# Loading the first adapter factors and one weight chunk of a fused LoRA and FFN kernel in other pieces, on other queues

## The chip, the cores and the metric

The kernel runs on 1 core of one Trainium2 chip. The metric is the device time of the whole program in microseconds (us). The kernel before took 473.98 us, the median of 3 runs (473.75 to 474.29).

## The reference

For each of 8 batches of 256 tokens with 1024 features, a low-rank adapter chosen by an index is applied, its result goes through a feed-forward network whose inputs are rounded to fp8, and the input is added back:

```python
Bx  = einsum('bni,bri->bnr', x, B[ids])        # rank 16
h   = einsum('bnr,bor->bno', Bx, A[ids])
g   = fp8(h) @ gate_w.T ;  u = fp8(h) @ up_w.T  # 1024 -> 2752
out = x + fp8(silu(g) * u) @ down_w.T           # 2752 -> 1024
```

## The kernel before

**Tiling.** The 2048 tokens are four blocks of 512 (t = 0 to 3), each of two batches. Features are eight groups of 128 (k = 0 to 7). The 2752 hidden features are 22 chunks (c = 0 to 21) of 128. TensorE takes a 128x128 piece of weights and streams 512 tokens past it: 16 such matmuls for one chunk and one block (eight k for gate, eight for up).

**Start.** While the first transfers are under way TensorE multiplies ones (`warm`, L523). Block 0 goes first: `two_times_b` (L549) makes `bx` = B x, eight matmuls for each k, in the order of k; two small `warm` matmuls stand before k 7 and six behind it. VectorE and ScalarE copy `bx` to `bm`. `two_times_a` (L618) makes `c` = A `bm` in 32 short matmuls of 32 rows for each half, and both engines round `c` to fp8 as `xg`. Then `gate_up(0, 0)` runs, and from there on TensorE goes from chunk to chunk.

**What is loaded, and in which order.** Nearly all loads are issued by SyncE (SP); a few by ScalarE (ACT) and GpSimd (POOL). x of block 0 comes in four pieces: k 0 and 1, k 2 to 4, k 5 and 6, k 7 (L432, L433, L441, L442). B of batch 0 goes out on ScalarE's queue (L434), B of batch 1 on SP (L440). `touched` (L436) is a 1 KB read of the weights into a scrap tile. A of the two batches goes into one tile, `a_two[0]`, whose 128 rows are cleared by GpSimd (L384): `load_a_two` (L398) brings 48 rows of 2 KB for each batch, 16 rows for one half of the output, 16 rows that the host has filled with zeros, and 16 rows for the other half. Both go out on SP behind all of x. Then come gate and up weights, 1 MB for each chunk: chunks 0 and 1 in two halves, 2 to 4 whole (L445).

**Block 1.** Seven chunks (0 to 6) are used first for block 0 alone. There are five weight buffers, so chunk 5 is loaded when chunk 0's buffer is free and chunk 6 when chunk 1's is. Chunk 6 is loaded in two halves with all of block 1's x between them: half of chunk 6 (L770 to L772), x k 0 to 6 (1792 KB), x k 7 (256 KB), the other half. In chunk 6 the rows stand gate k 0 to 7, then up k 0 to 7 (`GATE_FIRST`). `gate_up(6, 0)` runs the gate matmuls of k 0 to 3 first; then `two_times_b_in_parts` makes `bx` of block 1 (L790), which needs block 1's x; then come gate k 4 and 5, up, and so on. x of blocks 2 and 3 (2 MB each) and their A and B follow on SP.

**Later.** For the other blocks chunks 0 and 1 are loaded again, and chunks 7 to 21. `NSPLIT = 3` makes chunks 7, 8 and 9 come in two halves.

**Queues.** An engine issues its instructions in order. The program uses eight completion semaphores for the DMAs of SP and ScalarE, in turn: a DMA that takes one again first waits until the DMA that had it has landed.

Of the kernel before, what the change touches and what calls it, by code (L numbers as in the profile page):

```python
# [23 lines left out]
H = 1024  # L24
I = 2752
R = 16
NH = H // P
# [7 lines left out]
NAHEAD = 2  # L35
NHELD = NFIRST + NAHEAD

NSPLIT = 3

GATE_FIRST = (1, NHELD - 1)  # L40

# [25 lines left out]
def x_of(x4, t, k):  # L67

    first = 0
    for n in PIECES[t]:  # L70
        if k < first + n:
            break
        first += n
    at = (t * NH + first) * P * TB
    piece = x4[at : at + n * P * TB].rearrange("(p k n) -> p k n", p=P, k=n)
    return piece, first
# [18 lines left out]
def gate_up_of(w_gu, c):  # L95
    at = c * 2 * NH * P * P
    return w_gu[at : at + 2 * NH * P * rows_of(c)].rearrange("(p n) -> p n", p=P)
# [204 lines left out]
def adaln_ffn(  # L302
# [15 lines left out]
    nc = tc.nc  # L318
# [45 lines left out]
    with ExitStack() as fast:  # L364
# [5 lines left out]
        xs = [acts.tile([P, NH, TB], F32, name=f"x{t}") for t in range(NTB)]  # L370
# [8 lines left out]
        b_two = [lora.tile([P, 2 * BROW + R], F32, name=f"b{t}") for t in range(2)]  # L379
        a_two = [lora.tile([P, H // 2], F32, name=f"a{t}") for t in range(2)]  # L380
# [7 lines left out]
        def adapter_of(batch, queue):  # L388
            return queue.value_load(ids_i[0:1, batch : batch + 1], min_val=0, max_val=7)  # L389

        def load_b(b, i, adapter, queue):
            load = queue.dma_start(  # L392
                out=b[:, i * BROW : (i + 1) * BROW], in_=b8[bass.ds(adapter * P, P), :]
            )
            if queue is nc.gpsimd:
                tc.keep_in_program_order(load)

        def load_a_two(j, adapter):  # L398
            row = 2 * 32 * j + R * j
            nc.sync.dma_start(  # L400
                out=a_two[0][row : row + 3 * R], in_=a8[bass.ds(adapter * 3 * R, 3 * R), :]
            )

        def load_a_twice(a, q, src, part, queue):
            load = queue.dma_start(
# [5 lines left out]
        def load_x(t, k):  # L411
            piece, first = x_of(x4, t, k)
            ks = slice(first, first + piece.shape[1])
            nc.sync.dma_start(out=xs[t][:, ks, :], in_=piece)  # L414

        w_of = {}

        def load_gate_up(c, parts=1, between=()):
            n = NH if c == NI - 1 else 2 * NH
            w = wpool.tile([P, 2 * NH, P], F32, tag="w", name="w_gu")[:, :n]  # L420
            src = gate_up_of(w_gu, c).rearrange("p (k n) -> p k n", n=P)
            n //= parts
            for i in range(parts):
                nc.sync.dma_start(out=w[:, bass.ts(i, n)], in_=src[:, bass.ts(i, n)])  # L424
                if i == 0:
                    for load in between:
                        load()
            w_of[c] = w
# [2 lines left out]

        load_x(0, 0)  # L432
        load_x(0, 2)  # L433
        load_b(b_two[0], 0, adapter_of(0, nc.scalar), nc.scalar)  # L434
        touched = const.tile([R, R], F32, name="touched")
        nc.scalar.dma_start(  # L436
            out=touched, in_=gate_up_of(w_gu, 0).rearrange("(r g) n -> r g n", r=R)[:, 0, :R]
        )
        second = adapter_of(1, nc.sync)
        load_b(b_two[0], 1, second, nc.sync)  # L440
        load_x(0, 5)  # L441
        load_x(0, 7)  # L442
        load_a_two(1, second)
        load_a_two(0, adapter_of(0, nc.sync))
        for c in range(NFIRST):  # L445
            load_gate_up(c, parts=2 if c < 2 else 1)
        adapters = [adapter_of(2 + q, nc.gpsimd if q < 2 else nc.sync) for q in range(6)]
        lane = const.tile([P, 1], I32, name="lane")
        nc.gpsimd.iota(lane, pattern=[[0, 1]], base=0, channel_multiplier=1)
# [127 lines left out]
        def two_times_b_in_parts():  # L577

            n = SEQ // 2
            bx = [psum.tile([P, n], F32, tag="ps", name=f"bx{half}") for half in range(2)]
            times_b([bx[q // 2] for q in range(4)], b_twice[0], n, quads_of_two(1))
            bm = lora.tile([P, 2, n], F32R, name="bm_parts")
            rest = in_place_of_hid(NI - 11, [P, 2, n], F32R, "rest")
            held = tc.keep_in_program_order
            own = [slice(64 * half, 64 * (half + 1)) for half in range(2)]
            for half, copy in enumerate((nc.vector.tensor_copy, nc.scalar.copy)):
                held(copy(bm[own[half], half], bx[half][own[half]]))
            for half in range(2):  # L590
                held(
                    nc.vector.tensor_tensor(
                        rest[own[half], half],
                        bx[half][own[half]],
                        bm[own[half], half].bitcast(F32),
                        ALU.subtract,
                    )
                )
            for part, half in ((bm, 1), (bm, 0), (rest, 0), (rest, 1)):
                held(nc.scalar.copy(part[own[1 - half], half], part[own[half], half].bitcast(F32)))  # L600
            return [part.rearrange("p h n -> p (h n)") for part in (bm, rest)]
# [52 lines left out]
        def two_times_a_part(bms, part):  # L654
            round_two(1, part, times_a_parts(bms, a_parts[0], 2 * part), cut=1 + part)
# [11 lines left out]
        def four_times_a(bms, i):  # L667
            cs = times_a_parts(bms, a_parts[1 + i // 2], 2 * (i % 2))
            for q in range(4):
                to = xg[2 + q // 2][:, 2 * i : 2 * i + 2, bass.ts(q % 2, SEQ)]  # L670
                round_to(to, cs[q], nc.vector if q % 2 else nc.scalar)
# [81 lines left out]
        two_times_a(bm)  # L753
        gate_up(0, 0, turns=(2, 2, 2, 2))
        load_gate_up(NFIRST)
        tc.keep_in_program_order(nc.gpsimd.tensor_copy(b_two[1][:1, :1], w_of[2][:1, 0, :1]))
        for j in range(2):
# [10 lines left out]
        for c in range(NFIRST + 1, NHELD - 1):  # L768
            load_gate_up(c)
        load_gate_up(  # L770
            NHELD - 1, parts=2, between=(lambda: load_x(1, 0), lambda: load_x(1, NH - 1))
        )  # L772
        for t in (2, 3):
            load_x(t, 0)
# [8 lines left out]
        for c in range(2, NHELD - 1):  # L783
# [5 lines left out]
            between={  # L789
                4: lambda: bms.append(two_times_b_in_parts()),  # L790
                10: lambda: two_times_a_part(bms[0], 0),
            },
        )
        gate_up(NAHEAD, 1, turns=(4, 1, 1, 1, 1), between={5: lambda: two_times_a_part(bms[0], 1)})
        for c in range(NAHEAD + 1, NHELD - 2):
# [7 lines left out]
            between={  # L803
                8: lambda: four_times_a(bms[1], 2),
                14: lambda: four_times_a(bms[1], 3),
            },
# [2 lines left out]
            for t in (2, 3):  # L809
                gate_up(c, t)  # L810
        for c in (*range(NAHEAD), *range(NHELD, NI)):
            load_gate_up(c, parts=2 if NHELD <= c < NHELD + NSPLIT else 1)
            if c == NI - 2:
                nc.sync.dma_start(out=wt, in_=w_d_tail)
            for t in range(1 if c < NAHEAD else 0, NTB):
                gate_up(c, t)
# [71 lines left out]
        for k in range(NH - 1):  # L888
# [23 lines left out]
            first = k % 2 == 0  # L912
# [133 lines left out]
```

## Time and profile before

| | us |
|---|---|
| median of 3 runs | 473.98 |
| lowest, highest | 473.75, 474.29 |
| the profiled execution's own time | 473.92 |
| its span | 472.3 |
| TensorE busy in the span | 467.6 (99%) |
| VectorE, ScalarE, GpSimd busy | 106.6, 194.8, 16.0 |

The span runs from the first to the last instruction that the profiler saw. Engines are PE (TensorE matmuls), PEld (TensorE weight loads), DVE (VectorE), ACT (ScalarE), POOL (GpSimd) and SP (SyncE); a "q" behind an engine's name stands for its instruction queue, which is where DMAs are issued. Times in views are microseconds from the start of the span. An entry such as "[0.28 <-DMA x<-x]" says that the engine sat idle for 0.28 us and that a transfer of x ended that.

### The profile page before, as it was taken

The page shows a single profiled execution, that of the slowest core. Times are in us where ns is not written, and L with a number is a line of the kernel's source. Part 1 is how long each engine was busy: PE and PEld are TensorE (multiplying, and loading weights), DVE is VectorE, ACT ScalarE, POOL GpSimd, SP SyncE. Part 2 cuts the span into 40 slices and gives each one's busy share as a digit, 9 for nine tenths or more (in the row PEclk, how much of TensorE's full clock was granted, in tenths as well). Part 3 has the DMA queues.
Part 4 walks back from the last instruction along what each step waited for, and adds up shares of the span by engine and source line. Part 5 has one row for each costly group of instructions (what it writes and reads, how often), then busy time and mean ns, then how long its engine had stood idle before and what let it go on. Part 6 is the DMA issues. An engine that isn't in the chain of part 4 may idle for free.

```text
span 472.3 us, 5980 instructions
## 1 busy us (share of the span) xinstructions
PE 467.6 (99%) x2477; PEld 214.6 (45%) x2477; DVE 106.6 (23%) x170; ACT 194.8 (41%) x257; POOL 16.0 (3%) x32
## 2 busy tenths in 40 slices
PE   8999999999999999999999999999999999999997
PEld 5444444444444444444444444444444444444444
DVE  2314341222121212212122121231120111031031
ACT  2315258996655655453345545359112012021000
POOL 0230500000000000000000000000000000000000
PEclk9999999999999999999999999999999999999999
DMA  8999105352222201222221011132425345153031
GB/s 304 421 381 358 48 3 161 109 176 89 90 89 90 89 24 67 89 90 89 90 85 23 26 62 57 61 105 103 142 109 161 76 175 162 42 207 103 3 116 68
DMA packets 14661, 56.01 MB, mean 119 GB/s; under 512 B 1762, under 2 KB 2786, under 8 KB 12066
## 3 DMA queue, kind: packets, MB, share of 16 engines
q1 hardware_dynamic: 14256, 55.08, 34.0%
q8 instruction: 21, 0.34, 0.3%
q0 software_dynamic: 192, 0.40, 0.3%
q14 instruction: 14, 0.11, 0.1%
q10 hardware_dynamic: 178, 0.07, 0.1%
HBM read 47.15 MB, written 8.39 MB: 118 GB/s over the span
## 4 chain that ended last, share of the span: by engine, by line
PE 94%; DMA 4%; SPq 0%; issue 0%; DVE 0%
PE y L521 60%; PE yd L521 32%; DMA x<-x 4%; PE c L521 1%; PE bx L521 1%; DMA ids_i<-ids 0%; SPq L389 0%; PE warm L521 0%; SPq L392 0%; SPq L414 0%; DVE o L853 0%; SPq L424 0%; PE count L521 0%
## 5 line engine op out<-in xcount | busy, mean ns | idle before, releaser
L521 PE MATMUL y<-xg,w_gu 128*128 128x512 fp8e4 x1376 | 298.6, 379 | 0.0
L521 PEld LDWEIGHTS <-w_gu 128*128 128x128 bf16 x1376 | 133.7, 98 | 162.1 <-DVE xg L606 1.6
L521 PE MATMUL yd<-hid,w_d 128*128 128x512 fp8e4 (+2 forms) x693 | 146.0, 373 | 0.0
L695 ACT ACTIVATE g<-y,gate_s 128x512 f32<-128x512 f32 (+1 forms) x88 | 59.5, 681 | 134.1 <-PE y L521 134.1
L724 DVE SCALAR_TENSOR_TENSOR hid<-y,up_by_down,g 128x512 fp8e4<-128x512 f32 x84 | 63.1, 751 | 215.8 <-PE y L521 145.7
L521 PEld LDWEIGHTS <-w_d 128*128 128x128 bf16 x693 | 66.6, 98 | 78.9 <-issue 1.7
L507 ACT ACTIVATE junk<-w_d 128x1408 bf16<-128x1408 uint16 (+1 forms) x16 | 21.2, 1324 | 88.5 <-DMA w_d<-w_d 88.4
L853 DVE SCALAR_TENSOR_TENSOR o<-yd,down_s,x 128x512 f32<-128x512 f32 x28 | 20.0, 747 | 107.5 <-PE yd L521 93.9
L507 ACT ACTIVATE junk<-w_gu 128x2048 bf16<-128x2048 uint16 (+1 forms) x22 | 41.0, 1864 | 0.0
L514 ACT ACTIVATE junk<-hid 128x2048 bf16<-128x2048 fp8e4 x21 | 40.1, 1908 | 0.6
L514 ACT ACTIVATE junk<-xg 128x2048 bf16<-128x2048 fp8e4 x8 | 15.3, 1910 | 0.3
L606 DVE TENSOR_SCALAR xg<-c,inv 128x512 fp8e4<-128x512 f32 (+1 forms) x20 | 11.7, 638 | 6.4 <-PE c L521 6.4
L608 ACT ACTIVATE xg<-c,inv 128x512 fp8e4<-128x512 f32 (+1 forms) x20 | 10.6, 601 | 4.5 <-PE c L521 4.5
L521 PE MATMUL warm<-const-bfloat16-1.0 128*128 128x512 bf16 (+1 forms) x22 | 6.0, 430 | 0.9 <-PEq L1035 0.9
L853 DVE SCALAR_TENSOR_TENSOR o<-yd,down_s,xg 128x512 f32<-128x512 f32 (+2 forms) x5 | 3.2, 644 | 12.2 <-PE yd L521 9.8
L521 PEld LDWEIGHTS <-const-bfloat16-1.0 128*128 128x128 bf16 x23 | 2.3, 118 | 4.3 <-issue 4.0
L507 ACT ACTIVATION_READ_ACCUMULATOR junk<-w_gu 128x1 f32 x22 | 4.2, 193 | 0.0
L521 PE MATMUL yd<-hid_tail,w_dt 64*128 64x512 bf16 (+1 forms) x32 | 4.2, 377 | 0.0
L724 DVE SCALAR_TENSOR_TENSOR tail<-y,up_by_down,g 64x512 fp8e4<-64x512 f32 x4 | 3.0, 756 | 4.9 <-ACT g L695 4.8
L514 ACT ACTIVATION_READ_ACCUMULATOR junk<-hid 128x1 f32 x21 | 3.9, 187 | 0.0
L521 PE MATMUL bx<-x,b_four_twice 128*32 128x256 f32 x64 | 3.7, 381 | 0.0
L460 POOL TENSOR_SCALAR a_parts<-a_four,minus 128x512 fp32r<-128x512 f32 x2 | 3.1, 1564 | 1.7 <-DMA a_four<-a_twice 1.7
(69 smaller groups left out, 55.5 us busy)
## 6 DMA issues: line engine op xcount, KB each, us to landing
w_gu<-w_gu SPq DMA_DIRECT2D x17, 1024.0 KB, 4.9
outT<-o SPq DMA_DIRECT2D x31, 256.0 KB, 2.1
w_gu<-w_gu SPq DMA_DIRECT2D x13, 512.0 KB, 5.1
w_d<-w_d SPq DMA_DIRECT2D x8, 704.0 KB, 5.1
w_d<-w_d SPq DMA_DIRECT2D x8, 640.0 KB, 3.9
x<-x SPq DMA_DIRECT2D x2, 2048.0 KB, 20.0
x<-x SPq DMA_DIRECT2D x1, 1792.0 KB, 14.4
x<-x SPq DMA_DIRECT2D x2, 512.0 KB, 3.8
```

The source lines that it names most:

```text
L460: held(engine.tensor_scalar(parts, a, minus, None, ALU.mult))
L507: nc.scalar.activation(junk_like(w), low(w), AF.Copy, accum_out=lows[:rows, column : column + 1])
L514: nc.scalar.activation(junk_like(q), q, AF.Square, accum_out=squares[:rows, column : column + 1])
L521: tc.keep_in_program_order(nc.tensor.matmul(*args, **kwargs))
L606: nc.vector.tensor_scalar(to, c, scale, None, ALU.mult, saturate=False)
L608: nc.scalar.activation(to, c, AF.Copy, scale=scale, saturate=False)
L695: nc.scalar.activation(g[rows], gates, AF.Silu, scale=gate_s[: gates.shape[0]])
L724: nc.vector.scalar_tensor_tensor(to, in0=ups, scalar=up_by_down[rows], in1=g[rows], op0=ALU.mult, op1=ALU.mult, saturate=False,)
L853: nc.vector.scalar_tensor_tensor(o, in0=y, scalar=down_s, in1=x, op0=ALU.mult, op1=ALU.add)
```

## The change

`load_a_two` now brings only the rows that are not zero: two loads of 16 rows (32 KB) for each batch, in place of one of 48 rows (96 KB). The two of batch 1 stay on SP behind all of x. The two of batch 0 go out on ScalarE's queue, behind a one-element copy on ScalarE that reads x at k 2, and so waits for the piece k 2 to 4. SP no longer reads batch 0's index. Chunk 6 is loaded in three parts: a quarter (gate k 0 to 3), block 1's x, a quarter (gate k 4 to 7), then the half with up. Chunks 7 to 9 are loaded whole.

```diff
-NSPLIT = 3
+NSPLIT = 0
...
-        def load_a_two(j, adapter):
-            row = 2 * 32 * j + R * j
-            nc.sync.dma_start(
-                out=a_two[0][row : row + 3 * R], in_=a8[bass.ds(adapter * 3 * R, 3 * R), :]
-            )
+        def load_a_two(j, adapter, queue):
+            for g in range(2):
+                row = 32 * (2 * j + g) + R * j
+                tc.keep_in_program_order(
+                    queue.dma_start(
+                        out=a_two[0][row : row + R],
+                        in_=a8[bass.ds(adapter * 2 * R + g * R, R), :],
+                    )
+                )
...
-        def load_gate_up(c, parts=1, between=()):
+        def load_gate_up(c, parts=(0, 4), between=()):
...
-            n //= parts
-            for i in range(parts):
-                nc.sync.dma_start(out=w[:, bass.ts(i, n)], in_=src[:, bass.ts(i, n)])
+            cuts = [n * i // 4 for i in parts]
+            for i, at in enumerate(zip(cuts[:-1], cuts[1:])):
+                nc.sync.dma_start(out=w[:, slice(*at)], in_=src[:, slice(*at)])
                 if i == 0:
                     for load in between:
                         load()
...
-        load_b(b_two[0], 0, adapter_of(0, nc.scalar), nc.scalar)
+        first = adapter_of(0, nc.scalar)
+        load_b(b_two[0], 0, first, nc.scalar)
...
-        load_a_two(1, second)
-        load_a_two(0, adapter_of(0, nc.sync))
+        load_a_two(1, second, nc.sync)
+        tc.keep_in_program_order(nc.scalar.copy(touched[:1, :1], xs[0][:1, 2, :1]))
+        load_a_two(0, first, nc.scalar)
         for c in range(NFIRST):
-            load_gate_up(c, parts=2 if c < 2 else 1)
+            load_gate_up(c, parts=(0, 2, 4) if c < 2 else (0, 4))
...
         load_gate_up(
-            NHELD - 1, parts=2, between=(lambda: load_x(1, 0), lambda: load_x(1, NH - 1))
+            NHELD - 1,
+            parts=(0, 1, 2, 4),
+            between=(lambda: load_x(1, 0), lambda: load_x(1, NH - 1)),
         )
...
-            load_gate_up(c, parts=2 if NHELD <= c < NHELD + NSPLIT else 1)
+            load_gate_up(c, parts=(0, 2, 4) if NHELD <= c < NHELD + NSPLIT else (0, 4))
...
-        "a8": np.insert(a8, 1, 0, axis=1).reshape(8 * 3 * R, H // 2),
+        "a8": a8.reshape(8 * 2 * R, H // 2),
```

## Prediction

> **What bounds the kernel now.** I read the page's first part, then who makes TensorE wait, then the chain that ended last, then the first 45 us in order of time.
>
> ```profile
> PE 467.6 (99%) x2477; PEld 214.6 (45%) x2477; DVE 106.6 (23%) x170; ACT 194.8 (41%) x257; POOL 16.0 (3%) x32
> ```
>
> ```profile
> PE warm L521 <- PEq L1035: 0.9, 1, 0.9
> PE bx L521 <- DMA b<-b: 0.4, 1, 0.4
> PE bx L521 <- DMA x<-x: 0.3, 1, 0.3
> ```
>
> PE is busy 467.6 of 472.3 us, and in the waits it waits three times in all, 1.6 us. So the change has little to take. From the chain:
>
> ```profile
> 3.94 4.86 DMA x<-x
> 8.80 0.04 issue
> 8.84 0.43 PE bx L521 x8
> 9.27 0.46 PE warm L521 x6
> 9.72 0.04 issue
> 9.77 2.19 PE c L521 x61
> 11.96 7.03 PE y L521 x32
> ...
> 19.37 14.42 DMA x<-x
> 33.79 0.14 issue
> 33.93 1.96 PE bx L521 x64
> ```
>
> Two transfers are in it. The first is k 7 of block 0's x (landed 3.94 + 4.86 = 8.80). The second is the large piece of block 1's x (landed 19.37 + 14.42 = 33.79), and there PE stood, as its own order of time shows:
>
> ```profile
> 11.89 21.76 PE L521 MATMUL y<-xg,w_gu 128*128 128x512 fp8e4 x100
> 33.93 1.96 PE L521 MATMUL bx<-x,b_twice 128*32 128x128 f32 x64 [0.28 <-DMA x<-x]
> 35.81 1.47 PE L521 MATMUL y<-xg,w_gu 128*128 128x512 fp8e4 x6
> ```
>
> From 11.89 to 33.65 there are 100 matmuls at 0.218 us each and no gap; then 0.28 us idle for x. That figure hides a little, since a matmul's end is modelled. From the start of the last y (33.27) to that of the first bx (33.93) there are 0.66 us; at 50.45, where bx follows y without a wait, there are 0.31 (50.15 to 50.46). So x's lateness costs 0.35 us. After it no wait of PE is listed to the end.
>
> **The change part by part, against the profiled execution's 473.92 us.**
>
> *Chunk 6 in three.* Ahead of block 1's x stand 256 KB less of chunk 6. The DMA engines are full in this stretch:
>
> ```profile
> 19.40:33.80 14.40, 14.25 (x67) 6.26 (x64) 3.43 (x5) 2.75 (x4) 7.12 (x12) 1.00 1.03 389
> ```
>
> The last two columns are the DMA share (1.03) and GB/s (389). The piece was issued at 19.37 and took 14.42 us because of what stood before it in SP's queue. 262 KB at 389 GB/s are 0.67 us; the 64 KB of zero rows that go (2 x 16 rows of 2 KB) are another 0.17. So x lands at 33.79 - 0.84 = 32.95. PE wants it at 33.93 - 0.35 = 33.58. The stall of 0.35 goes entirely, with 0.6 us to spare. What is late next? The second quarter of chunk 6 (gate k 4 and on) is wanted when bx ends, about 35.5. The old second half was issued at 20.33 and landed 15.4 later at 35.73; the quarter now ends 256 KB and 64 KB sooner, 34.9. The up half lands at 35.73 - 0.17 = 35.56; it is wanted after gate k 4 to 7, 35.5 + 4 x 0.22 = 36.3. Both hold, with 0.6 to 0.8 us in hand. If that cover is gone (a slow DMA engine), each 0.1 us late is 0.1 us of stall. **-0.35 us.**
>
> *SP's later issues.* One more part moves each later DMA one semaphore on. x of block 2 now waits for chunk 3 in place of chunk 2, block 3's for chunk 6's first quarter in place of chunk 5 (27.63 before, about 29 now), and its B for block 1's x (about 33). At each of these moments the queue still holds more than the 2 MB of block 2 (landing 20.80 + 19.9 = 40.7), so the engines don't run dry and nothing lands later. The next to need them are GpSimd's copies, which end at 49.05 for a bx at 50.45: 1.4 us of cover, 0.35 of which the gain eats. **0.**
>
> *Start: x.* SP's issues through k 7 of x stay. The two loads on ScalarE's queue put 64 KB beside x. If both get ahead of x's k 7, that is two rows of 2 KB on each of 16 engines: 64 KB at 371 GB/s (the rate from 2 to 8.5 us) are 0.17 us, and k 7 is on the chain, one for one. Bounds 0 and +0.17; I take **+0.05**, since k 7 was issued at 3.94 and these can't be before 6.2.
>
> *Start: A.* Here is the risk. Today A is issued on SP at 4.64 and 5.80 and takes
>
> ```profile
> L400 SPq DMA_DIRECT2D a<-a x2: 330/342/355, 4.6 to 5.8; - x2
> ...
> DMA to landing us min/median/max: 3.8/3.8/3.8
> ```
>
> so the later one lands at 9.63, just before c starts at 9.77. But `warm` runs until 9.72 and the copies to `bm` end at 9.58 (VectorE) and 9.62 (ScalarE), so an earlier A gains at most 0.1 us. How late may it be? The list of the changed program's instructions with their waits shows what the loads wait for. On SP the first takes the semaphore that x k 2 to 4 had, which landed 4.85 after 1.29, at 6.14; so it goes out at 6.17 in place of 4.64, the second at about 6.55. On ScalarE the copy waits for the same x. I place the two issues at about 6.2 and 6.6 (one issue takes 0.35 to 0.39 there). Behind them on ScalarE stands only the copy to `bm` at 9.36. The price of such a load, from both sides: an output write in a quiet queue lands 2.0 us after issue, so 8.6; on ScalarE's queue under x's traffic B took 3.4 and `touched` 3.6, so 10.0 to 10.2; A on SP took 3.83, so 10.43. PE would start c late by 0 to 0.3, 0.5 or 0.7 us. The nearest rows are those of ScalarE's queue, and I go below them for a reason that the trace shows. `touched` and B had their first packets 2.65 and 2.30 us after issue, where a load in a quiet queue has it after 0.97 (the loads from 78.99 on); the rest, 1.68 and 1.33, is a wait behind x packets of 4 and 6 KB at 159 and 234 ns, some 6 to 9 packets. Now the packets in front are x's 2 KB at 84 ns: 0.5 to 0.75 us. So the last load's packets start at 6.6 + 0.97 + 0.65 = 8.2, and first packet to landing took 0.94 and 1.06 for those two rows: 9.2. On SP the two loads follow k 7 directly, with a third of the old rows each, and land by about 9.3. Gain or loss at c: **0** (bounds -0.1 to +0.7).
>
> The DMA page of the Trainium skill speaks against this part ("DMA: Bandwidth & Descriptors", section "Rules for kernel authors"): loads under 64 KB pay mostly overhead and should be joined, and spreading DMAs over queues wins no bandwidth. By that, four loads of 32 KB in place of two of 96 KB would save nothing of the 0.17 us, and the sum would be -0.13 in place of -0.30. The same page ("Queues, rings and completion order") has each DMA engine serve its queues in turn, one packet of several descriptors at a time, so that a load on ScalarE's queue would wait for at most what one SP packet holds; the waits of `touched` and B fit that, and by it A lands in time.
>
> *Start: weights.* SP's first weight loads are held up too. The first half of chunk 0 goes from 6.17 to about 6.95; chunk 1's first half waits for k 5 and 6 of x (3.46 + 4.38 = 7.84), its second for a ScalarE load (about 9, before 7.59), chunks 2 to 4 come 1 to 2 us later. What hides it: the engines still work off x and A until 8.4. Half of chunk 0 landed at 11.2 and is wanted at 11.9. Chunk 1's second half landed at 7.59 + 8.5 = 16.1 and is wanted after 24 matmuls, 11.89 + 24 x 0.218 = 17.1; its data can't start before chunk 0 and chunk 1's first half (1.5 MB, until about 12.5) are through, so an issue at 9.6 is early enough. Without that cover the price would be the 1 us by which a delay of 2 us oversteps 17.1. **0.**
>
> *The rest.* Chunks 7 to 9 whole: the first is loaded at 86 us and used after chunks 0 and 1 of three blocks (about 129), so nothing. The copy of one element and two more DMA issues lie on ScalarE's idle 6.65 us before 9.36. **0.**
>
> Sum: -0.35 + 0.05 = -0.30. 473.92 - 0.30 = 473.62; the median of the runs is 0.06 above the profiled one, so 473.7.
>
> **Rivals.**
>
> *A lands late, and c waits* (slower). One mechanism: the second ScalarE load, issued at 6.6, takes as long as rows of that queue did. The start loses what the load comes in after 9.7. The gain of 0.30 is used up at a landing of about 10.0, 3.4 us after issue, which is B's own time. At 3.6 it is 10.2: +0.5 - 0.3 = +0.2, 474.2. At the 4.86 us of x's k 7, 11.46: +1.75 - 0.3, 475.4. For it: two rows of the very queue. Against: packets in front are a third as long, and 32 KB is less than B's 68.
>
> *The stall stays* (the change doesn't do what it says). One of 16 DMA engines ends far behind the others at block 1's x: the first of its 16 completions came at 32.09, the last at 33.79. If that engine's lag comes from something other than bytes, x lands no earlier and only the start's +0.05 is left: 474.0. Against: its queue is served in order, and it too has 16 KB less before x.
>
> *A little more*: the stall goes, A comes 0.1 earlier and x is not touched: 473.92 - 0.45 = 473.5.
>
> **Chances.** Forecast 0.55, A late 0.22, the stall stays 0.13, a little more 0.10. Range: low end 473.5 less the 0.2 by which runs lie below the median; high end 473.92 - 0.35 + 0.17 + 0.7 = 474.4, rounded up to 474.5. A measurement of this kernel can tell about 0.2% (0.95 us) from no change. Faster by more needs 473.0, where no part reaches: 0.04. Slower by more needs 474.9, A about 1.2 us late: 0.08, out of the first rival. Same: 0.88.
>
> **What would show it.** In the changed profile: PE without a wait for x before block 1's bx, which starts at about 33.6; c starting at 9.8; the A loads landing before 9.7; y starting at 11.9 to 12.0; the second quarter and half of chunk 6 not waited for. A wait of c for A would prove the first rival, a wait of bx for x near 33.7 the second. I am wrong if PE waits anywhere that it doesn't today.

## The result and the profile after

The changed kernel takes 475.19 us (median of 22 runs, 474.29 to 476.45) where the kernel before took 474.08 (22 runs, 473.65 to 474.82). The ratio is 1.0021, with a 95% interval from 1.0015 to 1.0027. So the change costs about 1.1 us; the forecast was 473.7, and the time lies above its range, which ended at 474.5.

The profiled execution of the changed kernel took 474.52 us, near the low end of its runs, with a span of 472.6. Its totals look like those of before. First line of the page:

```profile
PE 468.1 (99%) x2477; PEld 214.6 (45%) x2477; DVE 106.6 (23%) x170; ACT 195.2 (41%) x258; POOL 16.0 (3%) x32
```

What makes TensorE wait (total us, times, longest):

```profile
PE warm L527 <- PEq L1043: 0.9, 1, 0.9
PE bx L527 <- DMA x<-x: 0.3, 1, 0.3
```

The wait for x that is left is that of block 0's k 7. The one for block 1's x, 0.28 us in the prediction's lines, is no longer listed. But x is not early: it landed at 34.01, where 32.95 was forecast, and bx started 0.16 us later, at 34.17. (Where bx does wait for it, it starts 0.13 to 0.14 us behind x's landing, 33.79 and 33.93 before.) And the chain that ended last (start, us, what) tells of something new:

```profile
1.30 4.94 DMA x<-x
...
6.26 0.07 ACT touched L449
...
6.43 3.18 DMA a<-a
...
9.63 0.33 SPq L428
...
10.01 9.34 DMA w_gu<-w_gu
...
19.39 14.85 PE y L527 x68
34.24 1.89 PE bx L527 x64
```

The old chain went through two loads of x. The new one goes through a weight load: chunk 2, issued at 10.01, landed at 19.34, and y of chunk 2 started right behind it. TensorE's own order of time shows no bracket at that place, because the wait is short and the end of a matmul is modelled:

```profile
12.21 22.03 PE L527 MATMUL y<-xg,w_gu 128*128 128x512 fp8e4 x100
34.17 1.96 PE L527 MATMUL bx<-x,b_twice 128*32 128x128 f32 x64
```

The starts tell it. Where nothing waits, the 100 matmuls need 21.69 us from the first y to block 1's first bx (this is so in six of the kernels below). Here it is 34.17 - 12.21 = 21.96: 0.27 us were lost at chunk 2. Before it was 22.04, 0.35 lost at x. The 0.27 are not a price of chunk 2 alone: had it come in time, x would still have held bx until about 34.15, by the 0.14 us above.

A second profile of the changed kernel (after_again below; 474.99 us) shows the same wait at a size that no one misses; x landed at 34.56 there, again just ahead of bx:

```profile
11.97 7.28 PE L527 MATMUL y<-xg,w_gu 128*128 128x512 fp8e4 x32
19.83 14.85 PE L527 MATMUL y<-xg,w_gu 128*128 128x512 fp8e4 x68 [0.58 <-DMA w_gu<-w_gu]
34.69 1.95 PE L527 MATMUL bx<-x,b_twice 128*32 128x128 f32 x64
```

From block 1's bx on the four profiles of the two kernels are equal to 0.02 us: 16.53 us to block 2's bx (which is that of block 3 too), 269.19 to the first `yd`, 149.43 to the last matmul. So in them one number holds what the change does inside the span: when block 1's bx starts. It is 33.93 and 33.64 in two profiles of before, 34.17 and 34.70 in two of after, 0.65 us later on average. Both profiles of after are quicker than most of its runs: the median span of the 22 is 473.3, against 472.25 to 472.5 in the medians of the runs of before made with the experiments. One more place where the time can go is shown by after_padded, below.

Another 0.25 us of the 1.1 lies outside the span: the time less the span is 1.80 to 2.01 us in the 22 runs of after, 1.90 in the median, and 1.65 to 1.68 in the medians of the runs of before. Among the experiments, those with A on ScalarE's queue and chunk 6 in three have it too (touched_on_pool, ungated, early_w, after_padded: 1.85 to 1.88); a_only has 1.71, and all others, c6_only and a_on_sp among them, have 1.64 to 1.73. No view shows what that is.

**Where the weights became late.** SP's own order of time, before:

```profile
4.64 1.49 SPq L400 DMA_DIRECT2D a<-a  x2
6.17 3.62 SPq L424 DMA_DIRECT2D w_gu<-w_gu  x7
```

and after:

```profile
3.94 0.43 SPq L418 DMA_DIRECT2D x<-x  x1
6.37 0.91 SPq L402 DMA_DIRECT2D a<-a  x2
7.33 4.79 SPq L428 DMA_DIRECT2D w_gu<-w_gu  x7
```

SP stands from 4.37 to 6.3 for the semaphore of x k 2 to 4, then issues two A loads, and only then the first weights: at 7.33 in place of 6.17. What that does to the DMA engines is seen in the stretch from 6 to 16 us, which the view cuts into 40 slices of 0.25 us; each digit is the busy share of the 16 engines in tenths. Before:

```profile
DMA  9989899999999799999999999999999999998899
DMA packets 1090, 3.85 MB, mean 385 GB/s; under 512 B 132, under 2 KB 140, under 8 KB 991
```

After:

```profile
DMA  7979999998699999987899993946969999999989
DMA packets 1029, 3.27 MB, mean 327 GB/s; under 512 B 162, under 2 KB 176, under 8 KB 992
```

Before, the engines are full nearly from end to end (7 tenths once, at 9.25). After, they have holes at 8.25 to 8.75 (8 and 6 tenths) and at 12.0 to 13.5 (down to 3 tenths), and in ten microseconds 0.58 MB less came in. Only 0.06 MB of that is the zero rows that A no longer brings. The other 0.52 MB is 1.35 us of transfer at the 385 GB/s of before, an estimate from these two lines. It is early weights. Everything behind them in SP's queue comes later for it: chunk 2, where TensorE first runs into the hole, and block 1's x behind that.

### The profile page after: what moved, and what is told of

Read it like the earlier page. It is cut to its first block, busy times and chain, and to the rows that moved or that the text cites. A ratio compares the mean times of both kernels' runs of the same rounds, so it can differ in the third digit from the quotient of the medians.

```text
span 472.6 us, 5984 instructions
## 1 busy us (share of the span) xinstructions
PE 468.1 (99%) x2477; PEld 214.6 (45%) x2477; DVE 106.6 (23%) x170; ACT 195.2 (41%) x258; POOL 16.0 (3%) x32
## 4 chain that ended last, share of the span: by engine, by line
PE 95%; DMA 4%; SPq 0%; DVE 0%; issue 0%; ACT 0%; ACTq 0%
PE y L527 62%; PE yd L527 32%; DMA w_gu<-w_gu 2%; PE bx L527 1%; DMA x<-x 1%; PE c L527 1%; DMA a<-a 1%; SPq L418 0%; DVE o L861 0%; SPq L428 0%; ACT touched L449 0%; ACTq L402 0%; PE count L527 0%
```

## The experiments

The theories that the runs were to tell apart:

- *The turn of the semaphores.* Two more DMAs on SP's and ScalarE's turn of eight put SP's first A load behind x k 2 to 4, and all weights behind that. Late weights make y wait, wherever A is.
- *ScalarE's queue.* A, or x k 7 beside it, comes late because two loads go on another queue than SP's, and c starts late.
- *The later issues.* Not the first weight load but chunk 1's second half and chunk 2, which wait for semaphores until 9.6 and 10.0, are too late.
- *Smaller loads, or where A lies.* Four loads of 32 KB are slow in themselves, or A's smaller tensor moves the other tensors in memory.

### Which half of the change costs: c6_only, a_only

c6_only is the kernel before with chunk 6 in three parts and nothing else. a_only is the changed kernel with chunk 6 in two halves and chunks 7 to 9 split again.

```diff
# c6_only, against before
... (load_gate_up takes the cuts, as in the change)
-            NHELD - 1, parts=2, between=(lambda: load_x(1, 0), lambda: load_x(1, NH - 1))
+            NHELD - 1, parts=(0, 1, 2, 4), between=(lambda: load_x(1, 0), lambda: load_x(1, NH - 1))
# a_only, against after
-NSPLIT = 0
+NSPLIT = 3
-            parts=(0, 1, 2, 4),
+            parts=(0, 2, 4),
```

> The kernel before with only chunk 6 in three (a quarter, block 1's x, a quarter, a half); A's loads and chunks 7 to 9 as before. Theory 1 (A's loads on ScalarE's queue make x's k 7 and A late) and theory 2 (the weight loads, issued up to 2 us later because their semaphores come from A's loads, make chunk 2 late): 473.7, that is 0.35 under before, with no wait of bx for x near 33.6. Rival 3 (the quarters of chunk 6, with 2 KB rows, or their place, are what costs): 474.6 or more, with a new wait behind 33.6.

> The changed kernel with chunk 6 in two halves and chunks 7 to 9 in halves, as before: A's part of the change alone. Theories 1 and 2: as slow as the changed kernel, 475.0 to 475.6; the wait of bx for block 1's x is there only as far as TensorE isn't late already. Rival 3: 474.1 or less.

c6_only: 474.38 us, ratio 1.0003 [0.9994, 1.0012]. a_only: 475.12, ratio 1.0023 [1.0014, 1.0032]. The whole loss is in the loads of A and what they move. In c6_only's profile there is no wait at block 1's bx (21.69 us from the first y), so the third part does what was forecast at that place; that it wins nothing measurable is taken up with before_again.

### Does ScalarE's queue cost: a_on_sp

All four A loads on SP, without the copy.

```diff
-        tc.keep_in_program_order(nc.scalar.copy(touched[:1, :1], xs[0][:1, 2, :1]))
-        load_a_two(0, first, nc.scalar)
+        load_a_two(0, adapter_of(0, nc.sync), nc.sync)
```

> The changed kernel with all four A loads on SP behind all of x, batch 1's first, and no copy on ScalarE. Theory 1: x's k 7 lands at 8.8 again, c starts at 9.8, and the time falls by 0.3 to 1 us, to 474.2 or under. Theory 2: chunk 1's second half and chunk 2 now wait for x's k 7 and the first A load, so they go out near 8.9 and 9.3 in place of 9.6 and 10.0 (before: 7.6 and 8.1); most of the loss stays, 474.6 to 475.1, as a wait for chunk 2 near 19.

475.11 us, ratio 1.0018 [1.0009, 1.0027], as slow as the change. Chunk 0 was issued at 7.29 here too. So the queue of batch 0's A isn't the cause of the loss inside the span (the 0.25 outside it is absent here). The chain that ended last goes through block 1's x again and not through a weight load:

```profile
19.71 14.70 DMA x<-x
34.41 0.14 issue
34.55 1.96 PE bx L526 x64
```

Of the 0.63 us lost between the first y and this bx, about 0.2 lie in front of chunk 2 and about 0.4 in front of bx. The start of c, which I had suspected, also falls: it is 10.09 after, but 10.07 in c6_only, whose start is that of before, and 9.83 in after_again. It moves with x k 7's landing (8.80 to 9.20 among these), and in c6_only with A's (9.94), from run to run.

### How much do profiles of one kernel differ: after_again, before_again

The two kernels as they are, profiled once more, without an edit.

> The changed kernel once more, for a second profile. Its runs lie between 474.3 and 476.5, and the first profile is of a quick one (474.52). Theory 1: c starts at 10.0 to 10.2 again. Theory 2: the wait for chunk 2 near 19 is there again and is the part that varies from run to run: 0.3 us to 2 us.

> The kernel before, for a second profile. Theory 2 (SP's later weight issues are what costs): weights' packets at about 160 ns from chunk 0's second half on, chunk 1's second half begins near 12.8 to 12.9, no wait of y; bx of block 1 at 33.8 to 34.0. If it shows slow packets in chunk 1 too, as the changed kernel does, they don't come from the change.

after_again: 474.99 us; 1.03 us lost between first y and block 1's bx, most of it at chunk 2 (the fence above). before_again: 473.62 us; 21.71 us from the first y to block 1's bx, so the stall of 0.35 that the forecast meant to win is hardly there (0.02). In this execution x landed at 33.50, and y ended when it did. The stall is a matter of the execution, not of every one. In c6_only's profile, whose 474.38 is the median of its runs, there is none, but c started 0.30 us later than in before's, which takes back most of what that wins. Whether the third part has to do with the later start isn't shown; nothing is issued differently up to there.

### Are the later issues the cause: hold_sp

The kernel before with a copy of 64 bytes on SP between the halves of chunk 1, which waits for x k 7. It leaves chunk 0 and chunk 1's first half where they were and holds the rest up as the change does.

```diff
+        held_at = const.tile([1, 16], F32, name="held_at")
+        def hold():
+            tc.keep_in_program_order(
+                nc.sync.dma_start(out=held_at, in_=xs[0][:1, NH - 1, :16])
+            )
-            load_gate_up(c, parts=2 if c < 2 else 1)
+            load_gate_up(c, parts=2 if c < 2 else 1, between=(hold,) if c == 1 else ())
```

> The kernel before, with one added 64-byte copy on SP between the halves of chunk 1, which waits for x's k 7; its result isn't used. A is untouched, SP issues chunk 1's second half at about 9.2 and chunk 2 at 9.7, as in the changed kernel, while chunk 0 and chunk 1's first half go out as before. Theory 2: 474.7 to 475.3, with y waiting near 17 or 19. Theory 1 (A's loads themselves, or ScalarE's queue): 474.0 to 474.3, and no wait of y.

Chunk 0 was issued at 6.21, chunk 1's second half at 9.59, chunk 2 at 10.20 (after: 7.33, 9.63, 10.01). Chunk 2 landed at 18.49, on time, and 21.77 us lie between y and bx. So in this execution the later issues opened no hole. The median is 474.62, ratio 1.0019 [1.0010, 1.0029]; the medians alone stand 1.0012 apart. The profile can't explain those 0.6 us, since it is of the quickest of the ten runs (474.21); they lie inside the span (472.95 in the median, before 472.35). This run doesn't take the later issues' part of the loss to nothing; ungated, below, speaks to it again.

### Late weights without touching A: dummy_two, two_on_sp

The kernel before, with A's loads as they were. dummy_two adds the copy and two 1 KB loads on ScalarE's queue, so that the turn of the semaphores is that of the change or worse (A itself goes out at 6.36 and 7.52 here, in place of 4.64 and 5.80). two_on_sp adds two 1 KB loads on SP between A and the weights.

```diff
# dummy_two, against before
+        tc.keep_in_program_order(nc.scalar.copy(touched[:1, :1], xs[0][:1, 2, :1]))
+        for i in range(2):
...
+                nc.scalar.dma_start(
+                    out=scrap,
+                    in_=gate_up_of(w_gu, 0).rearrange("(r g) n -> r g n", r=R)[:, 1 + i, :R],
+                )
# two_on_sp, against before
... (first is the index of batch 0, read as before)
+        for i in range(2):
+            scrap = const.tile([R, R], F32, name=f"scrap{i}")
+            tc.keep_in_program_order(
+                nc.sync.dma_start(
+                    out=scrap, in_=a8[bass.ds(first * 3 * R + 2 * R * i, R), :R]
+                )
+            )
```

> The kernel before, A's two loads of 48 rows on SP included, with the changed kernel's one-element copy and two more 1 KB reads of the weights on ScalarE's queue in the place of A's; their results aren't used. They shift the turn of the eight semaphores as the change does. Theory 2: SP issues chunk 0 at 7.3 and chunk 2 at 9.5 or later, and the time is 474.7 to 475.4. Theory 1: 474.0 to 474.3.

> The kernel before with two more loads on SP, of 1 KB each, between A's second load and chunk 0; their results aren't used. A's loads, queues and sizes are as before. SP issues chunk 0's first half at about 7.2 in place of 6.2, as in the changed kernel. Theory 5 (what costs is that chunk 0's first half goes out late, 7.3 in place of 6.2: the cold start of the weights' stream then isn't covered by x and A, and chunks 0 and 1 come about 1 us later): 474.8 to 475.3, chunk 1's second half begins at 13.7 or later in place of 12.8. If it is A's loads in their new form or on ScalarE's queue: 474.0 to 474.3.

dummy_two: 475.67 us, ratio 1.0040 [1.0026, 1.0054], chunk 0 issued at 7.90. two_on_sp: 475.68, ratio 1.0028 [1.0015, 1.0040]. SP in two_on_sp:

```profile
4.63 1.49 SPq L400 DMA_DIRECT2D a<-a  x2
6.33 0.85 SPq L449 DMA_DIRECT2D scrap<-a  x2
7.22 4.03 SPq L424 DMA_DIRECT2D w_gu<-w_gu  x7
```

A goes out when it always did; the weights go out 1.05 us later for two DMAs of 1 KB. And TensorE pays at y and at bx:

```profile
12.53 21.76 PE L529 MATMUL y<-xg,w_gu 128*128 128x512 fp8e4 x100 [0.54 <-DMA w_gu<-w_gu]
35.46 1.95 PE L529 MATMUL bx<-x,b_twice 128*32 128x128 f32 x64 [1.17 <-DMA x<-x]
```

The delay of the first weights alone, with A's loads where they were, makes a loss of the same kind and at least the same size. The bytes lost at 8 to 15 us come due at the first piece that TensorE needs soon (chunk 0 here, chunk 2 in the change) and at block 1's x behind them.

### The change with the old issue times: a0_on_pool, pool_later

Batch 0's two A loads on GpSimd's queue, which doesn't take part in the turn of the eight semaphores. In pool_later they stand behind a one-element copy that reads x k 0.

```diff
# a0_on_pool, against after
-        tc.keep_in_program_order(nc.scalar.copy(touched[:1, :1], xs[0][:1, 2, :1]))
-        load_a_two(0, first, nc.scalar)
+        load_a_two(0, adapter_of(0, nc.gpsimd), nc.gpsimd)
# pool_later, against after
-        tc.keep_in_program_order(nc.scalar.copy(touched[:1, :1], xs[0][:1, 2, :1]))
-        load_a_two(0, first, nc.scalar)
+        zeroth = adapter_of(0, nc.gpsimd)
+        seen = const.tile([1, 1], F32, name="seen")
+        tc.keep_in_program_order(nc.gpsimd.tensor_copy(seen, xs[0][:1, 0, :1]))
+        load_a_two(0, zeroth, nc.gpsimd)
```

> The changed kernel with batch 0's two A loads on GpSimd's queue, which has semaphores of its own, and no copy on ScalarE; SP's loads then take the semaphores that they had before, and are issued at the old times, chunk 2 at about 8. Theory 2: the loss is gone, 473.7 to 474.2, no wait of y; only x may come up to 0.2 later, since these loads go out near 3.5, ahead of x's k 5 to 7. Theory 1 (it is the loads of 16 rows, on whichever queue): 474.8 or more.

> The change with batch 0's two A loads on GpSimd's queue, behind a one-element copy on GpSimd of x k 0 (so that they go out at about 4.5 to 5, behind x's own issues, where they went out at 3.64 and 4.34 and held x k 7 up by 0.74 us before). Theory of the semaphores' turn: SP and ScalarE have the old count of DMAs, so chunk 0's first half is issued at 6.1 to 6.3, chunk 2 lands by 18.7, y runs into block 1's bx without a stall (21.7 us); x k 7 lands near 8.85, c starts at 9.8 to 10.1, bx of block 1 at 33.6 to 33.9: 473.6 to 474.2, ratio 0.999 to 1.0005. If the start of c is later still because A itself comes late on this queue, c starts above 10.3 and the time is 474.4 or more. Rival (four small loads cost the time wherever they are): 475, ratio 1.002.

a0_on_pool: 474.16 us, ratio 0.9999 [0.9989, 1.0009]. pool_later: 474.08, ratio 1.0003 [0.9994, 1.0012]. Both issue chunk 0 at 6.18 to 6.19, and neither has a wait between y and bx. The DMA engines in pool_later, 6 to 16 us, are full again:

```profile
DMA  9999899999899699999999999989999999999899
DMA packets 1095, 3.78 MB, mean 378 GB/s; under 512 B 164, under 2 KB 178, under 8 KB 996
```

Four small loads are not the cost, then. But they don't pay either. In a0_on_pool they went out at 3.64 and 4.34 and ran ahead of x k 7, which landed at 9.54 in place of 8.80, and c started 0.66 late; in pool_later they went out at 4.97 and 5.67, x k 7 landed at 9.12, c started 0.25 late. What they saved at bx (0.35) is spent there, wholly in a0_on_pool and for the greater part in pool_later.

### Where A lies in memory: after_padded, before_short

after_padded gives the changed kernel an A tensor of the old size, 768 KB. before_short gives the kernel before one of 512 KB (its loads then start at other rows, so that their contents are not those of A).

```diff
# after_padded, against after
-        "a8": a8.reshape(8 * 2 * R, H // 2),
+        "a8": np.pad(a8.reshape(8 * 2 * R, H // 2), ((0, 8 * R), (0, 0))),
# before_short, against before
-                out=a_two[0][row : row + 3 * R], in_=a8[bass.ds(adapter * 3 * R, 3 * R), :]
+                out=a_two[0][row : row + 3 * R], in_=a8[bass.ds(adapter * R, 3 * R), :]
-        "a8": np.insert(a8, 1, 0, axis=1).reshape(8 * 3 * R, H // 2),
+        "a8": a8.reshape(8 * 2 * R, H // 2),
```

> The changed kernel with 256 KB of unread rows at the end of A's tensor in HBM, so that this tensor is as large as before; not one instruction differs. Theory 4 (new: the tensor without zero rows is 256 KB smaller, what stands behind it in HBM moves, and with the weights where they now lie the DMA engines read chunk 1 slowly): packets of chunk 1 at 160 ns again, no wait of y for chunk 2, 473.7 to 474.3. Theory 2 (SP's later issues), or the loads of 16 rows themselves: 475.0 to 475.4, as the changed kernel.

> The kernel before with A's tensor in HBM 256 KB smaller, as in the change, and the same instructions; the loads of 48 rows start at row 16 x index in place of 48 x index, so what they bring isn't the adapter's A (the output differs for that), while sizes, queues and order stay. Theory 4: slow packets in chunk 1 between 11.5 and 13.5 and 474.7 to 475.2, though nothing is issued later. Theory 2 and the loads' form: 474.0 to 474.3, as before.

475.04 us, 1.0021 [1.0003, 1.0038], and 474.01, 1.0000 [0.9991, 1.0009]. Each keeps the time of the kernel that it came from; the place in memory is out. after_padded's profile (475.19) shows another cost. TensorE reached block 1's bx at 33.95, no later than before, but the bx of blocks 2 and 3 took 1.0 us longer than in the other profiles. After_padded, then after:

```profile
50.48 4.67 PE L527 MATMUL bx<-x,b_four_twice 128*32 128x256 f32 x64
50.70 3.66 PE L527 MATMUL bx<-x,b_four_twice 128*32 128x256 f32 x64
```

It needs copies of B that GpSimd makes once B, which is loaded behind block 3's x, has landed. They ended at 51.45, in the middle of this bx:

```profile
50.45 1.00 POOL L477 COPY b_four_twice<-b_four 128x128 f32<-128x128 f32 x4 [7.82 <-DMA b_four<-b]
```

Before they ended at 49.05, 1.40 us ahead of bx; with the change at 50.48 and 50.80 (after_again), 0.22 and 0.42 ahead. The instructions of after_padded are those of the change, so this wait belongs to it, in some executions.

### Earlier weights with A still on ScalarE's queue: touched_on_pool, early_w, ungated

touched_on_pool is the change with the 1 KB read of the weights on GpSimd's queue, one DMA less in the turn. early_w is the kernel before with chunk 6 in three, that read on GpSimd's queue, and batch 0's A (48 rows, one load) on ScalarE's behind the copy. ungated is touched_on_pool without the copy.

```diff
# touched_on_pool, against after
-        nc.scalar.dma_start(
+        nc.gpsimd.dma_start(
# ungated has this as well
-        tc.keep_in_program_order(nc.scalar.copy(touched[:1, :1], xs[0][:1, 2, :1]))
# early_w, against before (chunk 6 as in c6_only)
-        nc.scalar.dma_start(
+        nc.gpsimd.dma_start(
...
-        load_a_two(1, second)
-        load_a_two(0, adapter_of(0, nc.sync))
+        load_a_two(1, second, nc.sync)
+        tc.keep_in_program_order(nc.scalar.copy(touched[:1, :1], xs[0][:1, 2, :1]))
+        load_a_two(0, first, nc.scalar)
```

> The changed kernel with the 1 KB read into the scrap tile on GpSimd's queue, which takes one DMA out of the turn of the eight semaphores: SP's first A load no longer waits for x's k 2 to 4, and chunk 0's first half goes out at about 6.6, between before (6.2) and the change (7.3). Theory 5: most of the loss goes, 473.7 to 474.4, chunk 1's second half begins at 12.8 to 13.3. If it is A's loads in their new form or on ScalarE's queue: 474.9 to 475.3.

> The kernel before with chunk 6 in three, batch 0's A (48 rows, with the zeros) on ScalarE's queue behind the one-element copy, and the 1 KB read on GpSimd's queue: chunk 0's first half then goes out at about 5.1, earlier than before. Theory 5: no loss, 473.5 to 474.1; a gain, if any, is no more than the 0.35 of the wait for block 1's x. If ScalarE's queue is what costs: 474.6 or more.

> The change with the 1 KB read of the weights on GpSimd's queue and without the one-element copy, so that ScalarE issues A at about 3.5 to 4.5, ahead of all weights on SP. Theory of the semaphores' turn: chunk 0's first half is issued at about 6.7 (as in the run with that read alone moved), chunk 2 lands by 18.8, no stall between y and bx of block 1. Theory that a load on ScalarE's queue waits only for what was issued on SP before it: A lands by 9.6 and c doesn't wait for it; c starts at 9.8 to 10.3 (x k 7 may be up to 0.2 later for the 64 KB beside it), 473.8 to 474.4, ratio 0.9995 to 1.001. Rival (ScalarE's queue is slow in itself): A lands at 11 or later, c waits, 475 or more.

touched_on_pool: 475.29 us, ratio 1.0024 [1.0011, 1.0037]. early_w: 480.39, ratio 1.0120 [1.0087, 1.0152]. Both brought the weights forward (first issue 6.73 and 5.07), and here A did come late. From touched_on_pool's chain, the second A load on ScalarE's queue, issued 0.10 us behind chunk 0's second half on SP:

```profile
7.29 4.23 DMA a<-a
...
11.57 2.05 PE c L527 x60
```

and from early_w's, where A went out at 6.86, behind both halves of chunk 0 (5.07 and 6.48):

```profile
6.86 7.22 DMA a<-a
...
14.22 3.92 PE c L525 x64
```

Loads of 32 and 96 KB took 4.23 and 7.22 us; in the change itself, ahead of the weights, those of 32 KB took 2.8 to 3.2. ungated issues the same loads on the same queue at 3.60 and 4.13, ahead of all weights, and c waits for no A: 474.42 us, ratio 1.0004 [0.9993, 1.0015], chunk 0 issued at 6.50, chunk 2 landed at 18.55, 21.69 us from y to bx. Its chunk 1 halves and chunk 2 went out at 9.06, 9.44 and 9.91, as late as in the change, and nothing waited for them. That is the second run against the theory of the later issues. Its start of c, 10.22, goes with x k 7, which landed at 9.34 beside the two loads.

### All runs side by side

Sorted by the issue of the first weights. "MB" is what the DMA engines moved from 6 to 16 us, "chunk 2" its last landing, "y to bx" the time from the first y to block 1's bx (21.69 without a wait), "x to bx" the time from the landing of the large piece of block 1's x to that bx (0.13 or 0.14 where bx waited for it).

| | first weights issued | MB | chunk 2 | y to bx | x to bx | ratio |
|---|---|---|---|---|---|---|
| before_short | 6.16 | 3.81 | 18.55 | 22.07 | 0.13 | 1.0000 |
| before | 6.17 | 3.85 | 18.56 | 22.04 | 0.14 | |
| c6_only | 6.18 | 3.81 | 18.37 | 21.69 | 0.29 | 1.0003 |
| a0_on_pool | 6.18 | 3.79 | 18.41 | 21.69 | 1.09 | 0.9999 |
| pool_later | 6.19 | 3.78 | 18.56 | 21.69 | 0.60 | 1.0003 |
| hold_sp | 6.21 | 3.89 | 18.49 | 21.77 | 0.13 | 1.0019 |
| before_again | 6.22 | 3.78 | 18.43 | 21.71 | 0.13 | |
| ungated | 6.50 | 3.85 | 18.55 | 21.69 | 0.95 | 1.0004 |
| touched_on_pool | 6.73 | 3.69 | 18.59 | 21.69 (c waits) | 1.84 | 1.0024 |
| two_on_sp | 7.22 | 3.40 | 19.09 | 22.93 | 0.14 | 1.0028 |
| after_again | 7.26 | 3.31 | 19.78 | 22.72 | 0.13 | |
| after_padded | 7.26 | 3.39 | 19.11 | 21.69 (y starts late) | 0.17 | 1.0021 |
| a_on_sp | 7.29 | 3.38 | 19.27 | 22.32 | 0.14 | 1.0018 |
| a_only | 7.30 | 3.33 | 19.08 | 22.40 | 0.14 | 1.0023 |
| after | 7.33 | 3.27 | 19.34 | 21.96 | 0.16 | 1.0021 |
| dummy_two | 7.90 | 3.37 | 19.51 | 22.90 | 0.14 | 1.0040 |

The table falls into two groups with nothing between 6.73 and 7.22: first weights by 6.73, at least 3.69 MB and chunk 2 by 18.6; or from 7.22 on, at most 3.40 MB and chunk 2 at 19.1 or later. TensorE comes to chunk 2 at 18.9 to 19.2 (at 19.5 in two_on_sp, already late by chunk 0). In five of the seven profiles of the late group it is x that sets the start of bx in the end, and in after it would have done so 0.02 us earlier. So what costs is the lateness of the whole stream, and chunk 2 is only the place where TensorE first meets it.

early_w, held up by A at c, is left out, and it doesn't fit the first column: its first weights went out at 5.07, yet 3.44 MB came in from 6 to 16 us and chunk 2 landed at 19.70. A late first issue is the way in which the change lost its bytes; this run shows that there is another.

No version here beats the kernel before by anything that can be measured.

**What stays open.** That issuing late costs bytes is shown by two_on_sp and dummy_two. Why it costs so many is not. The first 4 KB weight packets start between 8.1 and 8.6 us in both groups of the table (9.0 in dummy_two). With the late issue the 16 engines then either stand idle (after, 12.0 to 13.5, though chunk 1's second half had been issued at 9.63) or handle the same packets in some 180 to 230 ns from 9 to 14 us (after_again, a_only), where before needs 160 to 170 from 10 us on; no view says which of the two causes the other. Nor is it explained where hold_sp's 0.6 us lie, what the 0.25 us outside the span is, or how often the wait of after_padded comes.

## Why the prediction was wrong, point by point

- **What bounds the kernel**: right. TensorE is busy to the end, and in the profiles of the two kernels whatever delays block 1's bx is passed on to the end.
- **Chunk 6 in three, -0.35**: the mechanism was right where the weights are on time (no wait at bx in c6_only), and the term was mis-sized. The stall was taken from one execution; in before_again it was 0.02, and the step by itself measures 1.0003 [0.9994, 1.0012]. x also came less early than forecast, 33.59 in c6_only where 33.79 - 0.67 = 33.12 was to be expected: its issue waits behind chunk 6 for chunk 1's buffer, and so moves with the start of y, which was 0.31 later there (12.19). In the change itself x landed at 34.01 and 34.56 where 32.95 was forecast, 0.16 and 0.13 us ahead of bx: what the third part moved forward the late weights moved back.
- **SP's later issues, 0**: the time held in the two profiles of the change (16.53 us from block 1's bx to block 2's, as before), but by luck. "Nothing lands later" was wrong: block 3's x landed at 49.05 in place of 47.72, and of the "1.4 us of cover" 0.22 and 0.42 were left. In after_padded the cover was gone, and the wait cost 1.0 us. Part of this comes from the third part of chunk 6 (0.76 left in c6_only), part from the late weights (0.47 in a_only).
- **Start: x, +0.05**: not separable. x k 7 landed 0.40 later in after's profile but 0.14 in after_again's, and 0.24 in c6_only's, which has no A beside it.
- **Start: A, 0**: right for this change; A landed at 9.44 to 9.97 and c wasn't held up by ScalarE's queue (a_on_sp is as slow). The forecast of 9.2 to 9.3 was 0.1 to 0.8 too early: the four loads went out at 6.37 to 6.99 and not at 6.17 to 6.6, and took 2.8 to 3.2 us. For the timely landing I drew on a queue served in turn by the packet (the Trainium skill, "DMA: Bandwidth & Descriptors", section "Queues, rings and completion order"), and put no time on such a packet. With the 9 to 17 descriptors that the page calls typical, at 160 ns for a 4 KB row here, one SP packet is an estimate of 1.4 to 2.7 us. Behind chunk 0 (1 MB) touched_on_pool's load paid 1.0 to 1.4 us more than such loads ahead of the weights (4.23 against 2.8 to 3.2), which is no more than that. The 7.22 us of early_w are, and the measurement decides. The other passage, that transfers under 64 KB pay mostly overhead ("Rules for kernel authors" of the same page), is in keeping with pool_later's 1.0003.
- **Start: weights, 0**: the step that failed. It saw the delay ("The first half of chunk 0 goes from 6.17 to about 6.95") and wrote it off ("the engines still work off x and A until 8.4"). The issue was at 7.33. A was also issued later, and from 8.25 to 8.75 the engines were already partly idle. The step then looked at each piece's own landing against its use and stopped at chunk 1. It didn't ask what the stream as a whole loses, and chunk 2, wanted at 18.9 to 19.2 and landing at 18.56 before, had only some 0.3 to 0.6 us in hand. The runs put the loss from 6 to 16 us at 0.52 MB; chunk 2 landed 0.8 to 1.2 us later than before, and block 1's x 1.1 to 1.6 later than forecast. The step named its price without cover, 1 us; 474.4 + 1 would have held the time. A cover that is argued and not shown belongs into the range with its price.
- **The rest, 0**: right.
- **Rivals.** "A lands late" is not what happened, though touched_on_pool and early_w show that it can. "The stall stays" is false for c6_only; in the change x does come late again, not for the lag of one DMA engine but for the weights ahead of it. The rival that was missing is the weights'. The sign named last, "I am wrong if PE waits anywhere that it doesn't today", is what the profile showed.

## What to carry to other kernels

Count the DMAs, not only their bytes: where completion semaphores are used in turn, one more small DMA moves every later DMA to another wait, and the large loads that follow on that engine may all leave later. When a transfer stream that TensorE follows closely is held up at its start, add up what the DMA engines moved over the whole stretch; the wait shows many microseconds later, at a piece that was itself issued in good time. Check every cover behind it too, in more than one profile: 1.4 us shrank to 0.2 here without a wait in either profile of the change. And before you count on the removal of a short stall, look at a second profile of the same kernel to see whether it is always there.

## What the runs showed of the hardware

- In two runs a small load didn't pass large ones that another engine had issued shortly before. On ScalarE's queue, 32 KB issued 0.10 us behind chunk 0's second half took 4.23 us, and 96 KB issued behind chunk 0 took 7.22; ahead of the weights 32 KB took 2.8 to 3.2 (after) or, beside x, 3.59 and 4.92 (ungated).
- Two DMAs of 1 KB put SP's next issue back by 1.05 us (two_on_sp, 6.17 to 7.22; SP waited for no semaphore in between) and, through the lost stream, cost some 1.3 to 1.6 us of the kernel's time (ratio 1.0028; medians 475.68 against 474.12).
- A wait of TensorE can cost more than its length. In early_w it stood 4.15 us before c, and then its granted clock was 0.50 from 14.2 to 18.1 us; the 64 matmuls of c took 3.92 us where they take 2.19.

```profile
14.20:18.10 3.90, 3.88 (x65) 3.68 (x66) 1.53 (x3) 1.51 (x4) 0.00 (x0) 0.50 1.05 431
```

The columns of this line of stretches are the stretch and its length, the busy time (and instructions) of PE, PEld, DVE, ACT and POOL, and then the granted clock, 0.50, the DMA share and GB/s.
